# Spreading a one-channel image with GpSimd, its chain over three engines, in the last layer of a fused kernel

## The chip, the cores and the metric

The kernel runs on one core of a Trainium2 chip. The metric is device time in microseconds (us) of one execution of the whole program, which holds four network layers. A core has TensorE (matmul, PE in the profile), VectorE (DVE), ScalarE (ACT), GpSimd (POOL) and SyncE (SP), which here issues nearly all DMA transfers. Each engine runs its instructions in the order of its own stream and waits on semaphores for the others. SBUF is the on-chip memory; PSUM is the small memory that TensorE writes to.

## The reference, cut to what matters

The input x has the shape (1, 256, 256, 128), float32. Each of four layers computes `x = x + layer(gn(x))`, where gn is a group norm. Layer 0 is triangle attention, layers 1 and 2 are triangle multiplications, and layer 3 is the convolution layer that the change touches:

```python
def c1(t):   # nine taps along a row, 128 channels -> 1 channel
    return lax.conv_general_dilated(t, w1, (1, 1), 'SAME', dimension_numbers=DN) + b1
w2c = w2[0, 4]
def c2(t):   # one 128x128 product per pixel
    return jnp.einsum('bhwc,cd->bhwd', t, w2c) + b2
t = relu(c1(x))
y = jnp.concatenate([x[:, :1], x[:, 1:] + t[:, :-1]], axis=1)
u = relu(c1(y))
z_main = u + jnp.roll(y, 1, axis=1)
z = jnp.concatenate([z_main[:, :H - 2], u[:, H - 1:H] + y[:, H - 2:H - 1], y[:, H - 1:H]], axis=1)
v = relu(c2(z))
p = jnp.concatenate([z[:, :, :1], z[:, :, 1:] + v[:, :, :-1]], axis=2)
r = relu(c2(p))
q_main = r + jnp.roll(p, 1, axis=2)
q = jnp.concatenate([q_main[:, :, :W - 2], r[:, :, W - 1:W] + p[:, :, W - 2:W - 1], p[:, :, W - 1:W]], axis=2)
return q
```

t and u have one channel. So z is the normalized x, moved down by one row, plus a one-channel image e = u + (t moved by rows) that is added to all 128 channels of a pixel.

## The kernel before, in words

The last layer keeps channels on the 128 partitions and pixels along the free axis. The 256 rows are cut into 32 chunks of R = 8 rows (2048 pixels). x arrives from DRAM (`x3T`), 1 MB per chunk, by `load9` (L1461), with nine buffers. One step s of the main loop (`for s in range(NR + 2)`) works on several chunks at once:

- `taps(s + 6)`: TensorE multiplies the chunk by the nine taps (p9_pp, L1467), ScalarE copies the result out of PSUM (p9_st, L1471), and SyncE stores it to DRAM (sD, four stores).
- The image works on blocks of 16 rows, two chunks, hence over two steps. `load_block` (L1486, odd steps) reads the taps back from sD in a layout that has rows over all partitions (p9_S). `sum_taps` (even steps) adds the nine shifted taps (L1506) into `acc`, whose one part gives t (add b1, mask by `inside`, relu: L1508, L1509) and whose other part is kept for u. `keep_t` stores t to DRAM (tD), `image_u` forms u from nine products of t and `wsum` (p9_prod, L1523 to L1527), `load_t` (L1516, at the start of the odd step) reads t back moved by a row, `image_e` (odd steps) adds u and that and stores e to DRAM (eD). `load_e` (L1544, at the start of the next even step, behind `load9`) reads the rows of e for two chunks, four loads of 4 KB, into one of two tiles p9_er.
- `start_z(s + 1)`: ScalarE writes the scaled and shifted x into the SBUF tile p9_z (L1554). `finish_z(s + 1)`: TensorE broadcasts the row of e to all partitions with `broadcast_rows` (four matmuls with a 0/1 selector, p9_eb in PSUM, L1087), and VectorE adds it to p9_z in two halves (L1568).
- `p_half(s)`, twice: TensorE's product of z with w2c (p9_pm, L1574) and VectorE's max and add (p9_pb, L1582). `q_half(s - 1)`, twice: the same product of p, and VectorE's L1596 and L1599 into p9_q. p9_q starts as a scaled copy of x made by ScalarE (L1673), and GpSimd's `residual` (L1588 to L1590) adds p moved by one column. ScalarE adds two single columns (L1671 in p9_pb, L1688 in p9_q).
- `emit(s - 2)`: sixteen TensorE transposes (p9_pt, L1611), two ScalarE copies (L1612), and one 1 MB store to the output (L1613).

The order on every engine is the program's order (`tc.manual_schedule()`): no planner moves instructions. SyncE issues all these transfers from one queue in that order and stops at the first whose data is not ready. PSUM is shared: p9_pp, p9_eb and p9_pt take turns in one pool of two buffers, `psX` (tag "x"); p9_pm has two buffers of its own.

Ahead of the loop, the first chunks and block 0 go through the whole chain, and steps 0 and 1 each take a block (`begin_image`, `end_image`) from start to end.

Of the kernel before, what the change touches and what calls it, by code (L numbers as in the profile page):

```python
# [16 lines left out]
P = 128  # L17
N = 256
# [14 lines left out]
def kernel(ctx: ExitStack, tc: tile.TileContext, a: dict, out: bass.AP):  # L33
# [1417 lines left out]
    with tc.tile_pool(name="p9", bufs=2) as sb, tc.tile_pool(name="p9psM", bufs=2, space=PSUM) as psM, tc.tile_pool(  # L1451
# [4 lines left out]
        ers = [sb.tile([P, CK], F32, name=f"p9_er{i}", bufs=1) for i in range(2)]  # L1456
# [6 lines left out]
        def taps(x, h0, n):  # L1463
# [6 lines left out]
            st = sb.tile([P, 2, N], F32, name="p9_st", bufs=3)  # L1470
# [31 lines left out]
        def sum_taps(b):  # L1502

            k = blocks[b]
            k["acc"] = sb.tile([P, 2 * BW + 8], F32, name="p9_acc")
            nc.vector.tensor_reduce(k["acc"], k["St"].rearrange("p k w -> p w k"), AX.X, ALU.add)  # L1506
            k["t"] = sb.tile([P, BW + 8], F32, name="p9_t")
            nc.vector.scalar_tensor_tensor(k["t"], k["acc"][:, BW:], b1, inside, ALU.add, ALU.mult)  # L1508
            nc.vector.tensor_scalar(k["t"], k["t"], 0.0, None, ALU.max)  # L1509
# [8 lines left out]
        def image_u(b):  # L1518
            k = blocks[b]
            t = k["t"][:, 0:BW]  # L1520
            nine = bass.AP(tensor=t.tensor, offset=t.offset, ap=[list(t.ap[0]), [1, BW], [1, TAPS]])
            prod = sb.tile([P, BW, TAPS], F32, name="p9_prod", bufs=1)
            nc.vector.tensor_tensor(prod, nine, wsum.unsqueeze(1).to_broadcast([P, BW, TAPS]), ALU.mult)  # L1523
            k["u"] = sb.tile([P, BW], F32, name="p9_u")
            nc.vector.tensor_reduce(k["u"], prod, AX.X, ALU.add)
            nc.vector.tensor_tensor(k["u"], k["u"], k["acc"][:, 0:BW], ALU.add)
            nc.vector.tensor_scalar(k["u"], k["u"], b1, 0.0, ALU.add, ALU.max)  # L1527

        def image_e(b):
            k = blocks.pop(b)  # L1530
            e = sb.tile([P, BW], F32, name="p9_e")
            nc.vector.tensor_tensor(e, k["u"], k["t2"], ALU.add)
            if b < NB - 1:
                nc.sync.dma_start(image_rows(eD, b * BR), e)
            else:
                nc.sync.dma_start(image_rows(eD, N - BR, BR - 2), e[0 : P - 16, :])
                nc.sync.dma_start(image_rows(eD, N - 2, 1), e[P - 8 : P, :])
                nc.sync.dma_start(image_rows(eD, N - 1, 1), k["t"][P - 8 : P, 4 : 4 + BW])

        def load_e(b):  # L1540

            e_chunks = eD.rearrange("o (s c h w) -> c (o s) h w", c=4, h=2, w=NP)
            for c in range(4):
                nc.sync.dma_start(  # L1544
                    ers[b % 2][32 * c : 32 * c + 2, :].rearrange("s (h w) -> s h w", h=2),
                    e_chunks[c, 2 * b : 2 * b + 2, :, 4 : 4 + N],
                )

        def start_z(s):

            zs[s] = sb.tile([P, R, N], F32, name="p9_z", bufs=3)

            def take(lo, hi, src):
                nc.scalar.activation(zs[s][:, lo:hi, :], src, AF.Identity, bias=k0, scale=r3)  # L1554

            take(0, 1, xs[s - 1][:, R - 1 : R, :] if s else xe[:, 1:2, :])
            if s + 1 < NR:
                take(1, R, xs[s][:, 0 : R - 1, :])
            else:
                take(1, R - 2, xs[s][:, 0 : R - 3, :])  # L1560
                take(R - 2, R, xs[s][:, R - 2 : R, :])

        def finish_z(s):
            eb = broadcast_rows(psX, ers[s // 2 % 2], s % 2, "p9_eb")
            zf = zs[s].rearrange("p h w -> p (h w)")
            for h in range(2):
                hs = slice(h * H2, (h + 1) * H2)
                nc.vector.tensor_tensor(zf[:, hs], eb[h], zf[:, hs], ALU.add)  # L1568
# [52 lines left out]
        for er in ers:  # L1621
            nc.gpsimd.memset(er, 0.0)
# [36 lines left out]
        for s in range(4, 8):  # L1659
            load9(s)  # L1660
        finish_z(0)
        for s in range(NR + 2):
            load9(s + 8)
            b = s // 2 + 2
            if s % 2 == 1 and 2 < b < NB:
                load_t(b)
            if s % 2 == 0 and 3 < b <= NB:
                load_e(b - 1)
            if s < NR:
                pbs[s] = sb.tile([P, R, N], F32, name="p9_pb")  # L1670
# [39 lines left out]
            if s > 1:  # L1710
                emit(s - 2)

# [181 lines left out]
```

## Time and profile before

| what | value |
|---|---|
| median of 4 runs | 3350.22 us (3349.19 to 3358.12) |
| profiled execution | 3355.72 us, span 3354.0, mean granted TensorE clock 0.958 |
| busy over the whole span | TensorE 3090.4 us (92%), VectorE 2269.7 (68%), ScalarE 2018.6 (60%), GpSimd 1661.2 (50%) |
| TensorE's share of the chain that ended last | 40% of the span (DMA 4%, VectorE 2%, GpSimd 2%) |
| first p product, p(0) | starts at 2958.94 us |
| last copy of an output tile | ends at 3345.4 us |

The busy shares are means over four layers with different limits. What the changed stage is limited by has to be read from its own stretch, roughly 2920 to 3354 us. The chain that ended last is followed back from the last instruction: each row says when a piece began, how long it lasted and on what engine, tensor and line it was. A group of instructions gives engine, line, output and inputs, the number, busy time, the mean time of one in ns, and the idle time before it with what ended that. SyncE's rows are issues of transfers: a long one is an issue that had to wait.

### The profile page before, as it was taken

Reading aid. Unit: us, or ns where it says so; the run is one execution under the profiler, and the core shown is the slowest. Engines: PE = TensorE matmul, PEld = TensorE weight load, DVE = VectorE, ACT = ScalarE, POOL = GpSimd, SP = SyncE. Lnnn points to the kernel's source line nnn. Section 1 sums busy time; section 2 is a strip of 40 time slices with the busy share of each in tenths; the row PEclk is TensorE's granted clock in tenths of the full one; section 3 lists DMA queues with packets and bytes.
Section 4 is the critical chain, followed back from the end, with each engine's and each line's share of the span. In section 5 each row is a group of like instructions: output and inputs, shape, how many; then the busy total and the mean of one; then the engine's idle time right before and its main releaser. Section 6 shows DMA issues by size and latency. Waiting matters only on the chain.

```text
span 3354.0 us, 52187 instructions
## 1 busy us (share of the span) xinstructions
PE 3090.4 (92%) x20036; PEld 1644.1 (49%) x20036; DVE 2269.7 (68%) x2613; ACT 2018.6 (60%) x2209; POOL 1661.2 (50%) x904
## 2 busy tenths in 40 slices
PE   5668999999999999967996999999999999769998
PEld 4515555555555555532532444444899633224444
DVE  5626888888888888862555544545455688757776
ACT  3576777777777777734586544543444477736665
POOL 4055777777777777740385000000455588624444
PEclk7799999999999999989997999999999999879999
DMA  9982333333333333359599676865899899756764
GB/s 356 353 320 95 117 110 121 109 118 106 122 109 121 109 115 115 110 197 382 173 375 366 229 287 229 306 259 201 338 351 353 315 385 388 313 162 194 209 189 133
DMA packets 297908, 749.48 MB, mean 223 GB/s; under 512 B 74551, under 2 KB 145161, under 8 KB 248473
## 3 DMA queue, kind: packets, MB, share of 16 engines
q1 hardware_dynamic: 289719, 735.49, 61.3%
q0 software_dynamic: 7648, 9.55, 0.8%
q8 instruction: 161, 2.64, 0.3%
q10 hardware_dynamic: 288, 1.05, 0.1%
q14 instruction: 92, 0.75, 0.1%
HBM read 458.34 MB, written 287.64 MB: 222 GB/s over the span
## 4 chain that ended last, share of the span: by engine, by line
PE 40%; DMA 4%; DVE 2%; POOL 2%; issue 1%; ACT 1%; SPq 0%; ACTq 0%; DVEq 0%; POOLq 0%
PE p_pm L1172 13%; PE tp_z L1852 7%; PE p_pm L1335 6%; PE p_pm L1574 5%; PE tp_a L1841 2%; PE p_st L1129 2%; PE p_pt L1611 1%; POOL x L1035 1%; PE p_rk L1087 1%; PE p_pg L987 1%; PE p_eb L1087 1%; DMA p_er<-eD 1%; PE p_pz L1014 1%; PE p_pp L1467 1%; DMA p_x<-x3T 1%
## 5 line engine op out<-in xcount | busy, mean ns | idle before, releaser
L565 DVE TENSOR_TENSOR p_e<-p_S,triT 128x1024 f32<-128x1024 f32 x512 | 609.4, 1212 | 144.4 <-PE p_S L555 144.4
L575 POOL TENSOR_TENSOR p_es<-p_e 128x1024 f32<-128x1024 f32 x256 | 603.7, 2369 | 125.3 <-issue 64.9
L573 ACT ACTIVATE p_e<-p_e,mbT 128x1024 f32<-128x1024 f32 x512 | 552.0, 1138 | 61.4 <-DVE p_e L565 61.3
L1172 PE MATMUL p_pm<-p_zn,wf 128*128 128x512 f32 x1040 | 449.2, 593 | 2.7 <-ACT p_a L1207 1.9
L540 PE MATMUL p_mm<-p_xn,w 128*128 128x512 f32 x768 | 405.3, 611 | 0.3 <-DVE p_v L535 0.3
L1172 PEld LDWEIGHTS p_pm<-p_zn,wf 128*128 128x128 f32 x1040 | 196.7, 190 | 255.3 <-issue 247.8
L555 PE MATMUL p_S<-p_q,p_k 32*128 32x256 f32 x4096 | 295.5, 401 | 3.5 <-DVE p_e L565 3.3
L1588 POOL TENSOR_TENSOR p_q<-p_q,p_pb 128x2024 f32<-128x2024 f32 x32 | 144.2, 4505 | 253.3 <-DVE p_pb L1582 253.3
L555 PEld LDWEIGHTS p_S<-p_q,p_k 32*128 32x128 f32 x4096 | 186.0, 184 | 159.5 <-PE p_mm L531 91.7
L514 POOL TENSOR_TENSOR p_xn<-p_xn,p_rs 128x1024 f32<-128x1024 f32 x63 | 151.3, 2401 | 205.4 <-DMA p_rb<-rzD 146.2
L1262 POOL MEMSET k<- 128x512 f32 x1 | 0.5, 521 | 508.4 <-DVE p_zn L1165 508.4
L1852 PE MATMUL tp_z<-p_B,tp_at 128*128 128x256 f32 x1024 | 250.4, 388 | 0.8 <-DMA p_B<-bD 0.5
L588 PE MATMUL p_o<-p_e,p_v 128*32 128x256 f32 x4096 | 248.6, 383 | 0.0
L1293 POOL TENSOR_TENSOR k<-k,p_sq 128x512 f32<-128x512 f32 x128 | 163.2, 1275 | 159.2 <-ACT p_sq L1291 159.2
L1852 PEld LDWEIGHTS tp_z<-p_B,tp_at 128*128 128x128 f32 x1024 | 185.1, 191 | 23.2 <-DVE tp_at L1843 1.6
L540 PEld LDWEIGHTS p_mm<-p_xn,w 128*128 128x128 f32 x768 | 126.0, 190 | 104.6 <-issue 88.5
L1292 DVE TENSOR_TENSOR k<-tp_z,k 128x512 f32<-128x512 f32 x128 | 88.6, 692 | 127.0 <-ACT p_sq L1291 127.0
L588 PEld LDWEIGHTS p_o<-p_e,p_v 128*32 128x32 f32 x4096 | 120.3, 110 | 110.3 <-ACT p_g L546 41.5
L1289 ACT COPY p_K<-tp_z 128x512 f32<-128x512 f32 x128 | 75.1, 586 | 157.9 <-PE tp_z L1852 157.9
L546 ACT ACTIVATE p_g<-p_mm,bgh 128x512 f32<-128x512 f32 x128 | 88.0, 687 | 131.3 <-PE p_mm L540 131.3
L531 PEld LDWEIGHTS p_mm<-w,p_xn 128*128 128x128 f32 x1024 | 134.4, 191 | 61.1 <-issue 60.4
L544 ACT ACTIVATE p_k<-p_mm,cqkg 128x512 f32<-128x512 f32 x128 | 88.0, 688 | 125.1 <-PE p_mm L540 124.9
(376 smaller groups left out, 5989.9 us busy)
## 6 DMA issues: line engine op xcount, KB each, us to landing
p_x<-x2T SPq DMA_DIRECT2D x60, 1024.0 KB
x<-x1T SPq DMA_DIRECT2D x51, 1024.0 KB
p_x<-in_x_dram SPq DMA_DIRECT2D x32, 1024.0 KB
p_x<-xT SPq DMA_DIRECT2D x64, 512.0 KB
x2T<-x SPq DMA_DIRECT2D x32, 1024.0 KB
aD<-p_a SPq DMA_DIRECT2D x32, 1024.0 KB
bD<-p_b SPq DMA_DIRECT2D x32, 1024.0 KB
p_A<-aD SPq DMA_DIRECT2D x32, 1024.0 KB
```

The costliest lines, as they stand in the source:

```text
L514: nc.gpsimd.tensor_tensor(xn, xn, groups[g]["rs"], ALU.mult)
L540: nc.tensor.matmul(pm, lhsT=w, rhs=t["xn"][:, cs_], start=True, stop=True)
L555: nc.tensor.matmul(Ss[h // 2][:, h % 2, u, :], lhsT=t["k"][hp, r * N + u * P : r * N + (u + 1) * P], rhs=t["q"][hp, r * N : (r + 1) * N], ...
L565: nc.vector.tensor_tensor(e[:, :, 2 * p : 2 * p + 2, :].rearrange("p u h n -> p h u n"), Ss[p], triT[:, 2 * p : 2 * p + 2, :, :], ALU.add,)
L573: nc.scalar.activation(e[:, u, :, :], e[:, u, :, :], AF.Exp, bias=mbT[:, u, i : i + 1])
L575: nc.gpsimd.tensor_tensor(es, e[:, 0, :, :], e[:, 1, :, :], ALU.add)
L588: nc.tensor.matmul(t["o"][hp, r % 2, :], lhsT=t["v"][:, r * 2 + u, hp], rhs=e[:, u, h, :], start=(u == 0), stop=(u == 1),)
L1172: nc.tensor.matmul(pm[:, c, :], lhsT=wf2[:, i, :], rhs=zns[s][:, k * CK : (k + 1) * CK], start=True, stop=True)
L1293: nc.gpsimd.tensor_tensor(k2, k2, sq, ALU.add)
L1335: nc.tensor.matmul(pm[:, c, :], lhsT=w, rhs=src[:, k * CK : (k + 1) * CK], start=True, stop=True)
L1574: nc.tensor.matmul(pm[:, 2 * c : 2 * c + 2, :], lhsT=w2c, rhs=src[:, r : r + 2, :], start=True, stop=True)
L1852: nc.tensor.matmul(pz[:, t, :], lhsT=at[:, u, t * P : (t + 1) * P], rhs=Bc[:, u, :], start=(u == 0), stop=(u == 1))
```

## The change: what it does

- ScalarE's `start_z` writes to PSUM (p9_zp, two psX buffers, in pieces of 256, 768 and 1024 elements for an ordinary chunk) instead of p9_z. GpSimd's `partition_broadcast` spreads the row of e (2048 elements) to all partitions in an SBUF tile p9_eb (one buffer), called by `spread_e(s + 2)` behind `residual(s)`. VectorE's `finish_z` adds both into p9_z. The matmuls of `broadcast_rows` for e go, and the two p9_er tiles with their clearing become one tile with a row at partition 0, 32, 64 or 96; `load_e` makes two loads of 8 KB instead of four of 4 KB.
- The image chain is divided over three engines. VectorE: two reductions in `sum_taps` (41 and 33 columns of results, the second into a tenth column of p9_prod) and one over ten columns in `image_u`. ScalarE: the relus (`relu_t`, `relu_u`). GpSimd: the mask and the product (`shift_t`), and the sum e (`image_e`).
- `keep_t` and `load_t` now follow each other at the start of the odd step, `keep_e` and `load_e` at the start of the even step, ahead of its `load9`. So each load's issue comes directly behind the store that it must wait for.
- `start_z(s + 1)` comes before the first writing of p9_q, and the column of p9_q (L1688) comes at the end of the step's order on ScalarE.
- p9_st has two buffers instead of three, p9_acc one.

```diff
@@ -1453,7 +1453,8 @@
     ) as psX, tc.manual_schedule():
         x3r = x3T.rearrange("d (h w) -> d h w", w=N)
         xs, zs, pbs, qs, blocks = {}, {}, {}, {}, {}
-        ers = [sb.tile([P, CK], F32, name=f"p9_er{i}", bufs=1) for i in range(2)]
+        er = sb.tile([P, SC], F32, name="p9_er", bufs=1)
+        ebs, zps = {}, {}
 
         def load9(s):
             if s < NR:
@@ -1467,7 +1468,7 @@
                 nc.tensor.matmul(
                     pp[32 * c : 32 * c + 32, 0, :], lhsT=w1f, rhs=x[:, 2 * c : 2 * c + 2, :], start=True, stop=True
                 )
-            st = sb.tile([P, 2, N], F32, name="p9_st", bufs=3)
+            st = sb.tile([P, 2, N], F32, name="p9_st")
             nc.scalar.activation(
                 st[0 : 32 * n].rearrange("p h w -> p (h w)"), pp[0 : 32 * n, 0, :], AF.Identity, bias=s0[0 : 32 * n]
             )
@@ -1502,11 +1503,25 @@
         def sum_taps(b):
 
             k = blocks[b]
-            k["acc"] = sb.tile([P, 2 * BW + 8], F32, name="p9_acc")
-            nc.vector.tensor_reduce(k["acc"], k["St"].rearrange("p k w -> p w k"), AX.X, ALU.add)
+            St = k["St"].rearrange("p k w -> p w k")
+            k["acc"] = sb.tile([P, BW + 8], F32, name="p9_acc", bufs=1)
+            k["prod"] = sb.tile([P, BW, TAPS + 1], F32, name="p9_prod", bufs=1)
+            nc.vector.tensor_reduce(k["acc"], St[:, BW:, :], AX.X, ALU.add)
+            nc.vector.tensor_reduce(k["prod"][:, :, TAPS], St[:, 0:BW, :], AX.X, ALU.add)
+
+        def relu_t(b):
+            k = blocks[b]
             k["t"] = sb.tile([P, BW + 8], F32, name="p9_t")
-            nc.vector.scalar_tensor_tensor(k["t"], k["acc"][:, BW:], b1, inside, ALU.add, ALU.mult)
-            nc.vector.tensor_scalar(k["t"], k["t"], 0.0, None, ALU.max)
+            nc.scalar.activation(k["t"], k["acc"], AF.Relu, bias=b1)
+
+        def shift_t(b):
+            k = blocks[b]
+            nc.gpsimd.tensor_tensor(k["t"], k["t"], inside, ALU.mult)
+            t = k["t"][:, 0:BW]
+            nine = bass.AP(tensor=t.tensor, offset=t.offset, ap=[list(t.ap[0]), [1, BW], [1, TAPS]])
+            nc.gpsimd.tensor_tensor(
+                k["prod"][:, :, 0:TAPS], nine, wsum.unsqueeze(1).to_broadcast([P, BW, TAPS]), ALU.mult
+            )
 
         def keep_t(b):
             nc.sync.dma_start(image_rows(tD, b * BR + 1), blocks[b]["t"][:, 4 : 4 + BW])
@@ -1517,19 +1532,21 @@
 
         def image_u(b):
             k = blocks[b]
-            t = k["t"][:, 0:BW]
-            nine = bass.AP(tensor=t.tensor, offset=t.offset, ap=[list(t.ap[0]), [1, BW], [1, TAPS]])
-            prod = sb.tile([P, BW, TAPS], F32, name="p9_prod", bufs=1)
-            nc.vector.tensor_tensor(prod, nine, wsum.unsqueeze(1).to_broadcast([P, BW, TAPS]), ALU.mult)
             k["u"] = sb.tile([P, BW], F32, name="p9_u")
-            nc.vector.tensor_reduce(k["u"], prod, AX.X, ALU.add)
-            nc.vector.tensor_tensor(k["u"], k["u"], k["acc"][:, 0:BW], ALU.add)
-            nc.vector.tensor_scalar(k["u"], k["u"], b1, 0.0, ALU.add, ALU.max)
+            nc.vector.tensor_reduce(k["u"], k["prod"], AX.X, ALU.add)
+
+        def relu_u(b):
+            k = blocks[b]
+            nc.scalar.activation(k["u"], k["u"], AF.Relu, bias=b1)
 
         def image_e(b):
+            k = blocks[b]
+            k["e"] = sb.tile([P, BW], F32, name="p9_e")
+            nc.gpsimd.tensor_tensor(k["e"], k["u"], k["t2"], ALU.add)
+
+        def keep_e(b):
             k = blocks.pop(b)
-            e = sb.tile([P, BW], F32, name="p9_e")
-            nc.vector.tensor_tensor(e, k["u"], k["t2"], ALU.add)
+            e = k["e"]
             if b < NB - 1:
                 nc.sync.dma_start(image_rows(eD, b * BR), e)
             else:
@@ -1537,35 +1554,45 @@
                 nc.sync.dma_start(image_rows(eD, N - 2, 1), e[P - 8 : P, :])
                 nc.sync.dma_start(image_rows(eD, N - 1, 1), k["t"][P - 8 : P, 4 : 4 + BW])
 
+        def row_e(s):
+            at = 32 * (s % 4)
+            return er[at : at + 1, :]
+
         def load_e(b):
 
-            e_chunks = eD.rearrange("o (s c h w) -> c (o s) h w", c=4, h=2, w=NP)
-            for c in range(4):
+            for s in range(2 * b, 2 * b + 2):
                 nc.sync.dma_start(
-                    ers[b % 2][32 * c : 32 * c + 2, :].rearrange("s (h w) -> s h w", h=2),
-                    e_chunks[c, 2 * b : 2 * b + 2, :, 4 : 4 + N],
+                    row_e(s).rearrange("o (h w) -> o h w", w=N),
+                    eD.rearrange("o (h w) -> o h w", w=NP)[:, s * R : (s + 1) * R, 4 : 4 + N],
                 )
 
+        def spread_e(s):
+            if s < NR:
+                ebs[s] = sb.tile([P, SC], F32, name="p9_eb", bufs=1)
+                nc.gpsimd.partition_broadcast(ebs[s], row_e(s))
+
         def start_z(s):
 
+            zps[s] = [psX.tile([P, H, N], F32, name="p9_zp", tag="x") for _ in range(2)]
+
+            def take(lo, hi, src):
+                h = lo // H
+                nc.scalar.activation(zps[s][h][:, lo - h * H : hi - h * H, :], src, AF.Identity, bias=k0, scale=r3)
+
+            take(0, 1, xs[s - 1][:, R - 1 : R, :] if s else xe[:, 1:2, :])
+            take(1, H, xs[s][:, 0 : H - 1, :])
+            if s + 1 < NR:
+                take(H, R, xs[s][:, H - 1 : R - 1, :])
+            else:
+                take(H, R - 2, xs[s][:, H - 1 : R - 3, :])
+                take(R - 2, R, xs[s][:, R - 2 : R, :])
+
+        def finish_z(s):
             zs[s] = sb.tile([P, R, N], F32, name="p9_z", bufs=3)
-
-            def take(lo, hi, src):
-                nc.scalar.activation(zs[s][:, lo:hi, :], src, AF.Identity, bias=k0, scale=r3)
-
-            take(0, 1, xs[s - 1][:, R - 1 : R, :] if s else xe[:, 1:2, :])
-            if s + 1 < NR:
-                take(1, R, xs[s][:, 0 : R - 1, :])
-            else:
-                take(1, R - 2, xs[s][:, 0 : R - 3, :])
-                take(R - 2, R, xs[s][:, R - 2 : R, :])
-
-        def finish_z(s):
-            eb = broadcast_rows(psX, ers[s // 2 % 2], s % 2, "p9_eb")
-            zf = zs[s].rearrange("p h w -> p (h w)")
-            for h in range(2):
+            zf, eb = zs[s].rearrange("p h w -> p (h w)"), ebs.pop(s)
+            for h, zp in enumerate(zps.pop(s)):
                 hs = slice(h * H2, (h + 1) * H2)
-                nc.vector.tensor_tensor(zf[:, hs], eb[h], zf[:, hs], ALU.add)
+                nc.vector.tensor_tensor(zf[:, hs], zp.rearrange("p h w -> p (h w)"), eb[:, hs], ALU.add)
 
         def product9(src, h):
             pm = psM.tile([P, H, N], F32, name="p9_pm")
@@ -1618,8 +1645,6 @@
         nc.sync.dma_start(xe, x3r[:, N - 2 : N, :])
         for s in range(4):
             load9(s)
-        for er in ers:
-            nc.gpsimd.memset(er, 0.0)
         S0 = sb.tile([P, TAPS, 2 * BW + 8], F32, name="p9_S")
         nc.vector.memset(S0, 0.0)
 
@@ -1639,16 +1664,22 @@
         blocks[-1] = dict(St=S0)
         load_block(0)
         sum_taps(-1)
+        relu_t(-1)
+        shift_t(-1)
         nc.sync.dma_start(image_rows(tD, 0, 1), blocks.pop(-1)["t"][P - 8 : P, 4 : 4 + BW])
 
         def begin_image(b):
             sum_taps(b)
+            relu_t(b)
+            shift_t(b)
             keep_t(b)
             load_t(b)
 
         def end_image(b):
             image_u(b)
+            relu_u(b)
             image_e(b)
+            keep_e(b)
             load_e(b)
 
         begin_image(0)
@@ -1658,21 +1689,25 @@
         load_block(1)
         for s in range(4, 8):
             load9(s)
+        spread_e(0)
         finish_z(0)
+        spread_e(1)
         for s in range(NR + 2):
+            b = s // 2 + 2
+            if s > 3 and s % 2 == 0 and b <= NB:
+                keep_e(b - 1)
+                load_e(b - 1)
             load9(s + 8)
-            b = s // 2 + 2
-            if s % 2 == 1 and 2 < b < NB:
+            if s > 1 and s % 2 == 1 and b < NB:
+                keep_t(b)
                 load_t(b)
-            if s % 2 == 0 and 3 < b <= NB:
-                load_e(b - 1)
             if s < NR:
                 pbs[s] = sb.tile([P, R, N], F32, name="p9_pb")
                 nc.scalar.activation(pbs[s][:, :, 0:1], zs[s][:, :, 0:1], AF.Identity, bias=kcol[:, 0:1])
+                if s + 1 < NR:
+                    start_z(s + 1)
                 qs[s] = sb.tile([P, R, N], F32, name="p9_q", bufs=3)
                 nc.scalar.activation(qs[s], xs[s], AF.Identity, bias=kcol[:, 2:3])
-                if s + 1 < NR:
-                    start_z(s + 1)
                 p_half(s, 0)
                 p_half(s, 1)
                 del xs[s]
@@ -1685,30 +1720,33 @@
             if 0 < s <= NR:
                 q_half(s - 1, 0)
                 q_half(s - 1, 1)
-                nc.scalar.activation(
-                    qs[s - 1][:, :, N - 1 : N], qs[s - 1][:, :, N - 1 : N], AF.Identity, bias=kcol[:, 1:2]
-                )
                 del pbs[s - 1], zs[s - 1]
             if s < NR:
                 residual(s)
+                spread_e(s + 2)
             if s < 2:
 
                 for i in range(2):
                     taps(xs[4 + 2 * s + i], (4 + 2 * s + i) * R, 4)
                 load_block(s + 2)
             elif b < NB:
-                if s % 2 == 0:
-                    sum_taps(b)
-                    keep_t(b)
-                    image_u(b)
-                else:
-                    image_e(b)
+                sum_taps(b) if s % 2 == 0 else image_u(b)
             if s > 1 and s + LEAD < NR:
                 taps(xs[s + LEAD], (s + LEAD) * R, 4)
             if s > 1 and s % 2 == 1 and b + 1 < NB:
                 load_block(b + 1)
             if s > 1:
                 emit(s - 2)
+                if b < NB:
+                    if s % 2 == 0:
+                        relu_t(b)
+                        shift_t(b)
+                    else:
+                        relu_u(b)
+                        image_e(b)
+            if 0 < s <= NR:
+                last = qs[s - 1][:, :, N - 1 : N]
+                nc.scalar.activation(last, last, AF.Identity, bias=kcol[:, 1:2])
 
 
 def general_attention(tc, d, w, dram, stats1):
```

More of the change, by code (lines that the diff above doesn't have):

```diff
@@ L1549, in start_z @@
+        def spread_e(s):
+            if s < NR:
+                ebs[s] = sb.tile([P, SC], F32, name="p9_eb", bufs=1)
+                nc.gpsimd.partition_broadcast(ebs[s], row_e(s))
         def start_z(s):
-            zs[s] = sb.tile([P, R, N], F32, name="p9_z", bufs=3)
+            zps[s] = [psX.tile([P, H, N], F32, name="p9_zp", tag="x") for _ in range(2)]
             def take(lo, hi, src):
-                nc.scalar.activation(zs[s][:, lo:hi, :], src, AF.Identity, bias=k0, scale=r3)
+                h = lo // H
+                nc.scalar.activation(zps[s][h][:, lo - h * H : hi - h * H, :], src, AF.Identity, bias=k0, scale=r3)
@@ L1565, in finish_z @@
-            zf = zs[s].rearrange("p h w -> p (h w)")
-            for h in range(2):
+            zs[s] = sb.tile([P, R, N], F32, name="p9_z", bufs=3)
+            zf, eb = zs[s].rearrange("p h w -> p (h w)"), ebs.pop(s)
+            for h, zp in enumerate(zps.pop(s)):
                 hs = slice(h * H2, (h + 1) * H2)
-                nc.vector.tensor_tensor(zf[:, hs], eb[h], zf[:, hs], ALU.add)
+                nc.vector.tensor_tensor(zf[:, hs], zp.rearrange("p h w -> p (h w)"), eb[:, hs], ALU.add)
```

## The prediction

> **What bounds the kernel now.** I read the times and the whole page first. The profiled execution took 3355.72 us (span 3354.0 and 1.72 around it), 5.5 above the median of 3350.22. TensorE is busy for 92% of the span, and only the last layer, from about 2920 us on, is changed. So I read that stage in four views: the chain of waits, the groups of instructions, SyncE's queue, and the clock after idle time. The chain (start, length, what) shows two neighbouring steps of the main loop, the second one disturbed:
>
> ```profile
> 3114.14 3.44 PE p_pm L1574 x8
> 3117.58 1.07 PE p_eb L1087 x8
> 3118.65 3.63 PE p_pm L1574 x8
> 3122.28 1.00 PE p_pp L1467 x8
> 3123.28 1.74 PE p_pt L1611 x15
> 3125.02 5.08 DMA p_er<-eD
> 3130.23 1.62 PE p_eb L1087 x7
> 3131.84 5.33 PE p_pm L1574 x8
> 3137.17 1.00 PE p_pp L1467 x8
> 3138.16 1.91 PE p_pt L1611 x16
> ```
>
> An undisturbed step is all TensorE: 3.44 + 1.07 + 3.63 + 1.00 + 1.90 = 11.04 us, 22.08 for a pair. The disturbed one waits for the load of e (p_er), and its next products take 5.33 instead of 3.63. The product p(s) of step s starts at 3009.43 for s = 3, 3079.71 for 9, 3267.03 for 25 and 3328.13 for 31. From 9 to 25 a pair therefore lasts 187.32 / 8 = 23.4 us, 1.3 over the undisturbed pair.
>
> The groups of that stage (window 2800 to 3354; busy us, mean ns, idle before) give the prices:
>
> ```profile
> L1588 POOL TENSOR_TENSOR p_q<-p_q,p_pb 128x2024 f32<-128x2024 f32 x32 | 144.2, 4505 | 253.3 <-DVE p_pb L1582 253.3
> L1568 DVE TENSOR_TENSOR p_z<-p_eb,p_z 128x1024 f32<-128x1024 f32 x64 | 75.3, 1219 | 22.7 <-ACT p_z L1554 13.0 <-PE p_eb L1087 9.7
> L1087 PE MATMUL p_eb<-p_er,sel 32*128 32x512 f32 x256 | 42.3, 654 | 20.3 <-DMA p_er<-eD 18.1 <-ACT p_z L1554 2.1
> L1329 POOL PARTITION_BROADCAST p_rb<-rs__17908 x10 | 22.9, 2295 | 0.7
> L1590 POOL TENSOR_TENSOR p_q<-p_q,p_pb 128x8 f32<-128x8 f32 x32 | 7.3, 227 | 0.0
> ```
>
> The fourth is an operation that the change adds, in another stage. The third shows 20.3 us of TensorE idle before the broadcasts, 18.1 of it for the load of e.
>
> SyncE's queue in one pair (start, busy, what) shows the order of the transfers:
>
> ```profile
> 3084.14 0.41 SPq L1613 DMA_DIRECT2D out_dram<-p_o  x1
> 3084.59 1.84 SPq L1461 DMA_DIRECT2D p_x<-x3T  x1
> 3086.52 1.18 SPq L1516 DMA_DIRECT2D p_t<-tD  x1
> 3092.87 0.32 SPq L1534 DMA_DIRECT2D eD<-p_e  x1
> 3093.28 1.38 SPq L1476 DMA_DIRECT2D sD<-p_st  x4
> 3095.97 1.03 SPq L1486 DMA_DIRECT2D p_S<-sD  x2
> 3097.10 0.85 SPq L1613 DMA_DIRECT2D out_dram<-p_o  x1
> ```
>
> eD is held from 3087.70 to 3092.87: the small t2 load (p_t) lands only behind a 1 MB output and a 1 MB x, about 8.5 us after the output's issue. A small transfer behind large ones is late, and everything later in the queue waits too.
>
> **Part 1: the broadcast leaves TensorE.** The four matmuls (8 records) of a chunk, 1.07 us on the chain, go. A step's floor is 3.44 + 3.63 + 1.00 + 1.90 = 9.97 us; 8.97 without taps. GpSimd takes over: 2.295 per chunk by L1329. After each of those stood a gap of 1.17 to 1.25, which the wait for p_g explains; bounds of the added price 0 and 1.2, and I take 0, as the row is the same operation on the same shape. GpSimd's step: residual 4.505 + 0.236 + 0.227 = 4.97, broadcast 2.3, half of the image work. By L1588 against L1590, an element costs (4505 - 227) / (2024 - 8) = 2.12 ns, so the 297-element product takes 0.21 + 0.63 = 0.84, the mask 0.3, the e add 0.27: 0.7 per step. Sum 8.0, 9.2 with the extra: under 9.97. spread_e(s+2) stands behind residual(s), a whole step ahead of finish_z(s+2), so nothing waits for it in the steady state.
>
> The page "GPSIMD Engine Reference" of the Trainium skill (sections 3 and 4.1) speaks against this placement: two-input elementwise work belongs on VectorE, as GpSimd is about twice as slow. L1523, the same product on VectorE, took 0.469, against 0.84 estimated. By the page's factor it would be 0.94; either adds 0.4 to 0.5 us per pair to an engine with 2 us to spare per step, and nothing to the sum.
>
> **Part 2: ScalarE and VectorE.** z goes to PSUM in three pieces instead of two (0.4 + 1.9 becomes 0.4 + 0.8 + 1.0, by 1229 ns for a mean of two), and the two relus add 0.3 each per pair (as L1688, 301 ns). ScalarE's step: 0.32 + 2.3 + 2.0 + 0.69 + 2.03 + 0.3 + 0.3 = 7.9. VectorE loses the small image work and keeps z 2.4, pb 2.55, q 2.97 and about 0.95 of reductions: 8.9. Both under 9.97. Moving start_z ahead of the q initialisation gives z earlier (13.0 us of L1568's idle was for it); the q column at the end of the order is read only by the transposes a step later. The zp pair holds both psX buffers until finish_z: that ends about 7.1 after p starts (pb by 4.7, then 2 x 1.2), as the taps come due at 7.07 and the transposes at 8.07. Cost 0, within 0.5.
>
> VectorE's small two-input operation L1508 once took 3.40 us beside L1588 instead of 0.26. No operation with two SBUF inputs is left on VectorE in the loop: that stall in the start-up goes.
>
> **Part 3: stores and their loads on SyncE, the new wait.** The t2 load stands directly behind the tD store, the er loads behind the eD store, so SyncE stands still until each store has landed. Queued behind: taps' stores, loads of the taps, x, and output. The cycle of a pair, from an output's issue in an even step:
> - output, x, tD: before, t2 landed 8.5 after the output's issue at the same place. The even step's x load is issued only 1.8 before that output, so some of it is still under way: up to 0.8 more. Taken 9.3.
> - t2, four sD, their landing: 0.3 + 1.38 + 1.26 (the last sD issue to the p_S issue) + 0.2 = 3.1.
> - p_S (two loads, 1.03), output 0.85, eD: p_S packets last 1.9 and the output's 4.0, start 0.95 after the issue, and a small store needs 0.5 at its end (1.45 alone, less the 0.95): 7.3 to 7.4; 7.3.
> - two er loads 0.6, x 0.4, four sD 1.4: 2.4 to 2.5.
>
> Sum 22.2 us per pair, over TensorE's floor of 19.94. So the queue, not TensorE, becomes the bound, and TensorE idles 2.3 us a pair. Bounds: 20.5 (no leftover x, and each store 0.3 quicker) and 24.6 (each of the four landings 0.6 later, half the spread of the er stalls, 5.1 to 5.7, on each side doubled).
>
> TensorE idle of 1.65 us at 3059.07 was followed by a granted clock of 0.57 in this row (window 3060 to 3064):
>
> ```profile
> 3060.00:3064.00 4.00, 4.00 (x10) 1.51 (x5) 2.36 (x2) 0.00 (x0) 4.00 (x3) 0.57 0.74 216
> ```
>
> Such a step is 1.7 us longer (5.33 against 3.63). In a queue-bound pair 19.94 + 1.7 = 21.6 still fits into 22.2, so I charge nothing; if it did not hide, 8 pairs x 1.7 = 14.
>
> The page "TensorE: Matmul & The Clock Gate" (Part 1) says that the clock falls after an idle window of about 3.4 us. By the page idle of 2.3 us would cost nothing at all; the row above shows 1.65 to be enough. The sum is the same by both, the slow rival differs.
>
> **Part 4: start-up.** The p9_st buffers go from 3 to 2: the second chunk's taps wait for the first's stores, landed at about 2941.0, + 2.3. taps(2) and taps(3) now wait behind finish_z(0), as start_z(0) holds both psX buffers, and stand ahead of p(0): the image chain 0 passes through ScalarE and GpSimd (four handovers, 0.2 each) and two broadcasts of 2.3 come in, of which one is ahead of z(0). p(0) is about 6 later. tD(1) is queued behind x loads that start later, and the broadcast of chunk 2 behind residual(0). Against it stands the 3.4 us stall. p(3): + 4 to + 8, taken + 6. The tail, without image work, stays.
>
> **Sum.** Steps 3 to 9: the lead of the image is not yet used up; 6 x 9.97 = 59.8 against 70.3: - 10.5. Steps 9 to 25: 8 x 22.2 = 177.6 against 187.3: - 9.7. Steps 25 to 31: two more at 11.1, four at 8.8 to 8.97, 57.4 against 61.1: - 3.7. Start-up + 6, and 1.5 for the broadcast's extra price where it is exposed (between 0 and 5). Total - 16.4: 3355.7 becomes 3339.3, and taken off the median, 3334.
>
> **The rivals.**
> - TensorE stays the bound (queue quick enough, cycle at most 19.9). For: the transfers occupy only about 72% of the DMA time. Against: the order of the queue makes four landings serial. Steps 9 to 25 take 159.5 (- 27.8), 25 to 31 about 55 (- 6), 3 to 9 - 10.5, start-up + 4: - 40, 3310.
> - Slower: the queue cycle exceeds 24.5. One mechanism: each store waits behind a megabyte of other traffic, and its wait blocks the traffic that would refill the queue. For: eD's hold of 5 us above. Against: p_S and output are short enough by their packets. At 24.6, steps 9 to 25 take 196.8 (+ 9.5), 3 to 9 gain only 6, 25 to 31 gain 2, start-up + 8: + 9.5, 3360. It decides from about 23.6 on, where the other gains and the start-up cancel.
> - No net change: cycle 23.2. Steps 9 to 25 - 1.7, 3 to 9 - 8, 25 to 31 - 3, start-up and broadcast + 9.5: - 3, 3347.
>
> **How the numbers follow.** Queue-bound gain as summed 0.43, TensorE-bound 0.14, no net change 0.16, slower 0.27. A measurement tells about 0.2% (6.7 us) from no change: 3343.5 to 3357 is "same". Faster 0.57, same 0.15, slower 0.28. The likeliest case by itself spans 3322 to 3343; the range over the cases is 3314 to 3364.
>
> **What would show it.** Right: no p_eb on TensorE, L1574 pairs about 22 us apart, SyncE waiting for tD and eD stores in every pair, TensorE idle about 2 us per pair before p or the transposes, p(3) 4 to 8 us later. Wrong: idle before finish_z put down to the broadcast, a GpSimd busy over 10 us a step, pairs at 20 or above 23.5, or a half clock that adds to the pair.

## The result, and the profile after

The changed kernel takes 3356.74 us in the median (3348.25 to 3362.98, 32 runs) against 3350.85 (52 runs) before: ratio 1.0014 over all runs, 95% interval [1.0008, 1.0019]. That is within the 0.2% named as no change, but the interval excludes 1: a small loss, where a gain of 16.4 was forecast. The prediction said 3334.

Medians of the whole program hide where the time went, because the layers ahead of the changed stage also vary between executions: in the two profiles the stage begins 6.7 us apart. So the stage is cut at the starts of the products p(s) on TensorE and measured from the norm's last instruction (the reciprocal, L210), which ends the statistics that the stage needs. All numbers are us, from the profiled executions (span 3354.0 before, 3350.0 after):

| stretch | before | predicted after | after |
|---|---|---|---|
| L210 to p(3) | 81.8 | 87.8 | 87.2 |
| p(3) to p(9) | 70.3 | 59.8 | 65.0 |
| p(9) to p(25) | 187.3 | 177.6 | 194.8 |
| the same per pair of steps | 23.42 | 22.2 | 24.35 |
| p(25) to p(31) | 61.1 | 57.4 | 56.4 |
| p(31) to the end | 25.9 | 25.9 | 25.7 |
| stage | 426.3 | | 429.1 |

Steps 3 to 9 gain 5.3 and steps 25 to 31 gain 4.7; the start-up loses 5.4 and the loop 7.5. The stage is 2.8 longer in these two executions, while the medians are 5.9 apart; the other 3.1 is not traced to a place.

The chain of waits of this profile breaks off after three pieces, so TensorE's timeline takes its place (start, length, line, operation; in brackets the idle time before and what ended it):

```profile
3109.42 3.60 PE L1601 MATMUL p_pm<-p_z,w2c 128*128 128x512 f32 x8
3112.86 3.60 PE L1601 MATMUL p_pm<-p_pb,w2c 128*128 128x512 f32 x8
3116.39 1.06 PE L1468 MATMUL p_pp<-p_x,w1f 128*32 128x512 f32 x8
3117.38 1.97 PE L1638 MATMUL p_pt<-ident,p_q 128*128 128x128 f32 x16
3119.19 3.60 PE L1601 MATMUL p_pm<-p_z,w2c 128*128 128x512 f32 x8
3123.69 3.70 PE L1601 MATMUL p_pm<-p_pb,w2c 128*128 128x512 f32 x8 [0.90 <-DVE p_pb L1609]
3130.84 1.06 PE L1468 MATMUL p_pp<-p_x,w1f 128*32 128x512 f32 x8 [3.44 <-DVE p_z L1595]
3132.06 3.59 PE L1638 MATMUL p_pt<-ident,p_q 128*128 128x128 f32 x16 [0.16 <-DVE p_z L1595]
```

The broadcast is gone from TensorE and an undisturbed step is 9.77 us (3109.42 to 3119.19), so TensorE's floor is 19.54 a pair, a little under the predicted 19.94. But in every pair the taps (L1468) wait for z. The groups of the stage (window 2800 to 3354; busy us, mean ns, idle before) say for what, one link after the other:

```profile
L1595 DVE TENSOR_TENSOR p_z<-p_zp,p_eb 128x1024 f32<-128x1024 f32 x64 | 75.2, 1217 | 49.8 <-POOL p_eb L1572 49.8
L1572 POOL PARTITION_BROADCAST p_eb<-p_er x32 | 73.5, 2296 | 60.9 <-DMA p_er<-eD 46.6 <-ACT p_q L1710 6.2 <-DVE p_pb L1609 3.7
L1468 PE MATMUL p_pp<-p_x,w1f 128*32 128x512 f32 x256 | 42.2, 745 | 74.6 <-DVE p_z L1595 65.4 <-DMA p_x<-x3T 9.2
```

TensorE waits for z, z for the broadcast, the broadcast for the load of e. Before, TensorE waited for that load 18.1 us; now it is 46.6 on GpSimd. SyncE's queue shows why it is late, one pair from an even step's output to the next (t2 is the load of t back from tD, er the load of e's rows; a transfer lands when it is reported done):

```profile
3103.93 0.41 SPq L1640 DMA_DIRECT2D out_dram<-p_o  x1
3104.43 3.68 SPq L1462 DMA_DIRECT2D p_x<-x3T  x1
3108.21 0.60 SPq L1527 DMA_DIRECT2D tD<-p_t  x1
3114.11 0.32 SPq L1531 DMA_DIRECT2D p_t<-tD  x1
3114.52 1.38 SPq L1477 DMA_DIRECT2D sD<-p_st  x4
3117.14 1.03 SPq L1487 DMA_DIRECT2D p_S<-sD  x2
3118.23 1.90 SPq L1640 DMA_DIRECT2D out_dram<-p_o  x1
3120.22 2.07 SPq L1551 DMA_DIRECT2D eD<-p_e  x1
3125.03 1.27 SPq L1564 DMA_DIRECT2D p_er<-eD  x2
3126.34 0.44 SPq L1462 DMA_DIRECT2D p_x<-x3T  x1
3126.89 1.37 SPq L1477 DMA_DIRECT2D sD<-p_st  x4
3128.31 0.41 SPq L1640 DMA_DIRECT2D out_dram<-p_o  x1
```

Apart from the landings (of tD before 3114.11, of sD before 3117.14, of eD before 3125.03) the rows follow each other without a gap: here SyncE never stands still for an engine's work. Between 3080 and 3267 it waited 42.5 us for tD's landing, 20.0 for eD's and 9.1 for sD's. The long x and eD issues were not waiting for data: e had been ready since 3116.17, and x's buffer was last read a step earlier. (The profile's view of waits puts 15.7 us of the x issues to the taps L1468, but those taps read another chunk.) The likely reading, not tested by itself, is that the queue was taking them slowly. The pair lasts 24.38 here. Over eight pairs from 3080 on, the means of the four legs are 10.32 (output to t2), 3.15 (t2 to p_S), 7.49 (p_S to er), 3.25 (er to output): 24.21.

### The profile page after: what moved, and what is told of

It reads as the page before. It is cut to its first block, busy times and chain, and to the rows that moved or that the text cites. A ratio compares the mean times of both kernels' runs of the same rounds, so it can differ in the third digit from the quotient of the medians.

```text
span 3350.0 us, 51718 instructions
## 1 busy us (share of the span) xinstructions
PE 3050.2 (91%) x19780; PEld 1635.6 (49%) x19780; DVE 2242.2 (67%) x2532; ACT 2039.4 (61%) x2274; POOL 1755.5 (52%) x984
## 5 line engine op out<-in xcount | busy, mean ns | idle before, releaser
L531 PEld LDWEIGHTS p_mm<-w,p_xn 128*128 128x128 f32 x1024 | 134.4, 191 | 61.1 <-issue 60.4
L1211 DVE SCALAR_TENSOR_TENSOR p_b<-p_pm,b2w,p_b 128x1024 f32<-128x1024 f32 x64 | 82.1, 1283 | 118.6 <-PE p_pm L1172 104.1
```

What stands on the lines that cost most here:

```text
L531: nc.tensor.matmul(pm[:, k * D : (k + 1) * D], lhsT=t["xn"][:, b * P : (b + 1) * P], rhs=wf[:, 2 * D : 3 * D], start=True, stop=True,)
```

## The experiments

Theory Q: the queue's chain of landings sets the pair. Theory G: the new chain er, GpSimd's broadcast, finish_z, taps sets it, however the queue runs. A pair is always taken from p(9) to p(25) of one profiled execution; a measured time is the median of two to eight runs.

### The store ahead of the x load

```diff
+            if s > 3 and s % 2 == 0 and b <= NB:
+                keep_e(b - 1)
+            if s > 1 and s % 2 == 1 and b < NB:
+                keep_t(b)
+            load9(s + 8)
             if s > 3 and s % 2 == 0 and b <= NB:
-                keep_e(b - 1)
                 load_e(b - 1)
-            load9(s + 8)
             if s > 1 and s % 2 == 1 and b < NB:
-                keep_t(b)
                 load_t(b)
```

> Edit: in each step the store (tD or eD) is issued ahead of the 1 MB x load and its load (t2 or er) behind it; nothing else. Theory Q (SyncE's queue of four serial landings sets the pair at 24.35 us between p(9) and p(25)): the x load is issued while the store lands, so the cycle shortens to about 3.2 (t2 issue to p_S issue) + 7.5 (p_S issue to er issue, x inside) + 8.3 (er, four sD, output, tD landing behind x and output) = 19.0, under TensorE's 19.94. Pair 20 to 21 us, p(9) to p(25) 160 to 168 instead of 194.8, time 3322 to 3332. Theory G (the chain er load, GpSimd's broadcast, finish_z, taps sets the pair, wherever the stores stand): pair 23.5 to 25, time 3350 or more, as er now lands behind x, later by 3.

Measured: pair 20.79, p(9) to p(25) 166.4, time 3319.72, ratio to the kernel before 0.9919 [0.9904, 0.9933]. Its queue:

```profile
3099.28 0.32 SPq L1531 DMA_DIRECT2D p_t<-tD  x1
3099.69 1.38 SPq L1477 DMA_DIRECT2D sD<-p_st  x4
3102.63 1.03 SPq L1487 DMA_DIRECT2D p_S<-sD  x2
3103.75 0.78 SPq L1640 DMA_DIRECT2D out_dram<-p_o  x1
3104.62 2.69 SPq L1551 DMA_DIRECT2D eD<-p_e  x1
3107.37 1.09 SPq L1462 DMA_DIRECT2D p_x<-x3T  x1
3111.10 1.27 SPq L1564 DMA_DIRECT2D p_er<-eD  x2
3112.47 1.49 SPq L1477 DMA_DIRECT2D sD<-p_st  x4
3114.01 0.41 SPq L1640 DMA_DIRECT2D out_dram<-p_o  x1
3116.16 0.34 SPq L1527 DMA_DIRECT2D tD<-p_t  x1
```

The x load is issued at 3107.37, inside the wait for eD, and SyncE has idle time of its own at 3114.42 to 3116.16, where it waits for t. Theory Q holds; for theory G the broadcast would have kept the pair at 23.5 or more, though nothing about it was changed. The exchanged order is worth 33 us in the stage of the profiled executions (429.1 - 396.0), or 37 by the medians, which were not taken side by side (3356.74 - 3319.72).

### Loads that wait for no store

```diff
-            nc.sync.dma_start(t2, image_rows(tD, b * BR))
+            away = x3T[0:1, 0 : P * BW].rearrange("o (p w) -> p (o w)", w=BW)
+            nc.sync.dma_start(t2, image_rows(tD, b * BR) if b < 3 else away)
...
-                    eD.rearrange("o (h w) -> o h w", w=NP)[:, s * R : (s + 1) * R, 4 : 4 + N],
+                    eD.rearrange("o (h w) -> o h w", w=NP)[:, s * R : (s + 1) * R, 4 : 4 + N]
+                    if b < 3
+                    else x3T[0:1, s * SC : (s + 1) * SC].rearrange("o (h w) -> o h w", w=N),
```

Both loads:

> Edit: from block 3 on, the t2 and er loads read as many bytes from x3T, which is long finished, instead of tD and eD; so e is not the image's from there on, but every transfer stays and no load waits for a store. Theory Q: SyncE never stands still for a landing of tD or eD, the pair falls to TensorE's floor, 19.9 to 20.3, p(9) to p(25) 159 to 163. Theory G (broadcast chain or GpSimd's order): pair still 23 or more, as the broadcast and everything behind it is unchanged.

Measured: pair 20.22, p(9) to p(25) 161.8, 3307.05 us. As theory Q expected: within 0.3 of the predicted floor of 19.94 and 0.7 over the measured 19.54, with GpSimd's work unchanged. By itself this run does not exclude a chain through the image's data, as e no longer depends on t here; the queue's rows above, in which SyncE waits for landings and no engine, do.

The t2 load alone:

> Edit: from block 3 on, only the t2 load reads from x3T instead of tD, so e is not the image's from there on; the er load still waits for the eD store. Theory Q: of the measured cycle 10.4 + 3.2 + 7.5 + 3.3 the first leg (an output's issue to t2's issue) falls to issue times and the queue's own fullness, about 5: cycle about 19 to 20, so the pair is 20 to 21. If each landing costs by itself, the two waits are worth about 5.5 each over the floor. Theory G: pair 23 or more.

Measured: pair 22.73, 3332.73 us. Neither theory's number: the gain is 1.6, not 3.4 or more. The queue shows where the rest went:

```profile
3102.09 0.47 SPq L1532 DMA_DIRECT2D p_t<-x3T  x1
3102.66 1.46 SPq L1477 DMA_DIRECT2D sD<-p_st  x4
3108.52 1.03 SPq L1487 DMA_DIRECT2D p_S<-sD  x2
```

From the last sD issue to p_S it is now 4.40, where the changed kernel has 1.24 (3115.90 to 3117.14). The taps' stores land behind the same output and x that tD had waited for, and p_S waits for them. The wait moved to the next landing.

The er load alone:

> Edit: from block 3 on, only the er load reads from x3T instead of eD, so what is spread is not e; the t2 load still waits for the tD store. Seen before: with the tD wait gone, p_S waited instead, since the taps' stores then landed behind output and x (4.4 us), and the pair fell only to 22.73. Theory Q now: SyncE runs from p_S to tD without a landing, but tD lands behind p_S, output, x, output, x: 0.95 + 1.9 + 3.8 + 3.5 + 3.8 + 3.5 + 0.5 = 17.9 after p_S's issue, and 3.1 from t2 to p_S: cycle 21.0, pair 20.6 to 21.8. If both waits cost alike: about 22.7. Theory G: 23 or more.

Measured: pair 22.16, 3333.89 us. A gain of 2.2, a little under what was expected (21.8 at most). Each single wait taken away gives 1.6 or 2.2; together they give 4.1.

### The broadcast twice

```diff
                 nc.gpsimd.partition_broadcast(ebs[s], row_e(s))
+                nc.gpsimd.partition_broadcast(ebs[s], row_e(s))
```

> Edit: GpSimd broadcasts each row of e twice into the same tile, 2.3 us more per chunk. Theory Q: GpSimd has 15.6 of 24.4 us busy in a pair, and the broadcast lies outside SyncE's cycle: 20.2 busy, pair 24.2 to 24.8, start-up + 2 to 5, time + 2 to 9. Theory G: the broadcast lies on the path once or twice per pair, pair 26.6 to 29, p(9) to p(25) 213 or more, time + 25 or more.

Measured: pair 24.03, so 2.3 us more in front of each z costs the loop nothing. The groups of 3073 to 3265:

```profile
L1596 DVE TENSOR_TENSOR p_z<-p_zp,p_eb 128x1024 f32<-128x1024 f32 x33 | 38.9, 1219 | 34.3 <-POOL p_eb L1573 34.0
L1573 POOL PARTITION_BROADCAST p_eb<-p_er x16 | 36.8, 2299 | 1.4
```

VectorE waits 34.0 us for the broadcast, and that is no proof that the broadcast is the bound: the idle time is named after the last link, and the pair is as long as without it. The time was 3369.06, 12 more than the changed kernel, where 2 to 9 had been expected. It is lost outside the loop: p(3) comes 6.8 later, p(3) to p(9) takes 3.2 more, and p(25) to p(31), where the image's transfers end, 7.3 more (63.7). So there the broadcast does count.

### Only the stores' places, in the kernel before

```diff
-            load9(s + 8)
             b = s // 2 + 2
-            if s % 2 == 1 and 2 < b < NB:
-                load_t(b)
             if s % 2 == 0 and 3 < b <= NB:
+                keep_e(b - 1)
                 load_e(b - 1)
+            load9(s + 8)
+            if s % 2 == 1 and 2 < b < NB:
+                keep_t(b)
+                load_t(b)
```

with `keep_e` split from `image_e`, and `keep_t` taken out of the even step, in lines not shown.

> Edit: the kernel before, with nothing of the change but the stores' places: tD at the start of the odd step behind the x load and directly ahead of the t2 load, eD at the start of the even step directly ahead of the er loads, ahead of the x load. Theory Q: the same queue cycle as after the change, 24.35, plus 0.7 for four er loads instead of two (2.0 against 1.27): pair 24.3 to 25.5 against 23.42, p(9) to p(25) 194 to 204, time + 7 to + 17 against the kernel before. Rival N (the stores' places do no harm by themselves; what the change lost comes from GpSimd's work): pair 23.0 to 23.8, time within 5.

Measured: pair 24.30, and 3348.04 us, ratio 1.0007 [0.9997, 1.0018]. Two rows of its queue on each side of the waits:

```profile
3103.79 0.45 SPq L1512 DMA_DIRECT2D tD<-p_t  x1
3108.92 0.32 SPq L1516 DMA_DIRECT2D p_t<-tD  x1
...
3113.97 2.42 SPq L1538 DMA_DIRECT2D eD<-p_e  x1
3119.72 1.14 SPq L1548 DMA_DIRECT2D p_er<-eD  x4
```

The loop is that of the changed kernel within 0.05 us a pair, with TensorE still broadcasting. So 24.3 belongs to the order of the stores and their loads, and in it the broadcast's move off TensorE is worth nothing. The time was expected 7 or more higher, and was not measurably higher: p(9) to p(25) lost 7.1, but p(3) to p(9) took 66.7 instead of 70.3 in the profiled executions.

### The broadcast back on TensorE, with the store ahead

The edit restores the two p9_er tiles, the four er loads, z in SBUF and `broadcast_rows` in the kernel of the first experiment:

```diff
+            eb = broadcast_rows(psX, ers[s // 2 % 2], s % 2, "p9_eb")
             zf = zs[s].rearrange("p h w -> p (h w)")
-            for h, zp in enumerate(zps.pop(s)):
+            for h in range(2):
                 hs = slice(h * H2, (h + 1) * H2)
-                nc.vector.tensor_tensor(zf[:, hs], zp.rearrange("p h w -> p (h w)"), eb[:, hs], ALU.add)
+                nc.vector.tensor_tensor(zf[:, hs], eb[h], zf[:, hs], ALU.add)
```

> Edit: the changed kernel with the store ahead of the x load, and the broadcast of e back on TensorE (p9_er, four loads of 4 KB, z written to SBUF, as before the change). Theory Q: the queue is no longer the bound, so the pair is TensorE's floor with the broadcast, 22.08, plus at most 0.8: 22.1 to 22.9, time 3335 to 3347. So spreading by GpSimd is worth 1.3 to 2 us a pair, once the queue allows. Rival: GpSimd's broadcast costs what TensorE's saves; then the pair is 20.8 to 21.2 as with GpSimd.

Measured: pair 22.07, TensorE's floor with the broadcast (22.08) to 0.01 us; 3329.04 us. The time is 6 below the range that was expected; the start-up is shorter, p(3) at 78.6 against 87.0 with GpSimd's broadcast. With the queue out of the way the move to GpSimd is worth 22.07 - 20.79 = 1.28 a pair, and costs 8.4 in the start-up as the change arranges it.

### Half an output store

```diff
-            nc.sync.dma_start(
-                out_tok[s * SC : (s + 1) * SC, :].rearrange("(k p) d -> p k d", p=P), ot
-            )
+            part = out_tok[s * SC : (s + 1) * SC, :].rearrange("(k p) d -> p k d", p=P)
+            if s < NR - 1:
+                nc.sync.dma_start(part[:, 0 : SC // P // 2, :], ot[:, 0 : SC // P // 2, :])
+            else:
+                nc.sync.dma_start(part, ot)
```

> Edit: the changed kernel, but each output store writes only the first half of its chunk (0.5 MB instead of 1 MB; the other half of the output is left unwritten); order and waits are untouched. Theory Q in its sharper form (a landing is late by the megabytes that stand in front of it): the output's packets shrink by 1.9 in each of two legs, cycle 24.35 - 3.8 = 20.5, pair 20.2 to 21.3. Rival L (a landing has a price of its own, whatever stands in front of it): pair 23.5 to 24.4.

Measured: pair 19.97, 3310.22 us. An even step's output and the one behind it:

```profile
3090.94 0.41 SPq L1642 DMA_DIRECT2D out_dram<-p_o  x1
...
3098.83 0.32 SPq L1531 DMA_DIRECT2D p_t<-tD  x1
...
3108.64 1.27 SPq L1564 DMA_DIRECT2D p_er<-eD  x2
...
3111.92 0.41 SPq L1642 DMA_DIRECT2D out_dram<-p_o  x1
```

Output to t2 is 7.89 here instead of 10.18. Over the first eight such pairs the means are 7.90 and 5.68 for the two legs that hold an output, 2.4 and 1.8 less, while t2 to p_S (3.15) does not move. So a landing is late by the bytes in front of it; the price per byte is not fixed by this one size, and with TensorE's floor so near the pair may have been held there.

### ScalarE's column, and the buffers of p9_st

On the kernel with the store ahead, the column back at its old place:

```diff
+                last = qs[s - 1][:, :, N - 1 : N]
+                nc.scalar.activation(last, last, AF.Identity, bias=kcol[:, 1:2])
                 del pbs[s - 1], zs[s - 1]
...
-            if 0 < s <= NR:
-                last = qs[s - 1][:, :, N - 1 : N]
-                nc.scalar.activation(last, last, AF.Identity, bias=kcol[:, 1:2])
```

> Edit: on top of the store ahead of the x load, ScalarE's column of p_q back at its old place, behind the q products' issue and ahead of taps' copy. With the queue out of the way this would show. GpSimd's residual of the step before ends about 2 us after p's start, and ScalarE would come to the column at about 6.4, so it waits for nothing: pair 20.6 to 21.0, within 0.2 of 20.79, time within 3 of the kernel it stands on. Rival: the column waits for GpSimd and holds up the taps' copies: pair 21.5 or more.

Measured: pair 20.71, 3318.78 us. It cost nothing, as charged.

```diff
-            st = sb.tile([P, 2, N], F32, name="p9_st")
+            st = sb.tile([P, 2, N], F32, name="p9_st", bufs=3)
```

> Edit: on top of the store ahead of the x load, p9_st with three buffers again. The prediction charged two buffers with + 2.3 in the start-up: p(0) at 33.0 to 34.0 after the norm's reciprocal instead of 35.7, p(3) at 84 to 85.5 instead of 87.0; the loop unchanged (20.79). Rival: the wait is hidden by the image chain of block 0, p(3) at 86.5 to 87.5.

Measured: p(0) at 33.8, p(3) at 84.7, pair 20.72. p(0) is 1.9 earlier than with two buffers and p(3) 2.3. The first is clear (seven profiles with the same start-up have p(0) at 35.7 to 36.3), the second hardly (p(3) at 85.7 to 88.9); in the time (3320.06) they are below what three runs can tell.

### The start-up

```diff
             taps(xs[s], s * R, 4)
-        start_z(0)
...
         load_block(0)
+        for s in range(2, 4):
+            taps(xs[s], s * R, 4)
         sum_taps(-1)
...
         begin_image(0)
+        start_z(0)
         end_image(0)
-        for s in range(2, 4):
-            taps(xs[s], s * R, 4)
         load_block(1)
```

with p9_st's three buffers and the store ahead of the x load.

> Edit: on top of the store ahead of the x load, the start-up: taps(2) and taps(3) stand behind load_block(0) and ahead of the image chain of block 0, start_z(0) between begin_image(0) and end_image(0), and p9_st has three buffers again. Theory on the start-up (p(0) 4.8 later through p9_st with two buffers and through taps(2), taps(3) behind finish_z(0)): p(0) at 30.5 to 32.5 after the norm's reciprocal instead of 35.7, p(3) at 82 to 84.5 instead of 87.0, time 2.5 to 5 less than without the edit, 3315 to 3317. Rival: the start-up is bound by x's loads and the image chain of blocks 1 and 2; p(3) stays at 86 to 88.

Measured: 3306.18 us, ratio to the kernel before 0.9878 [0.9862, 0.9895], the fastest version that computes the whole layer. p(0) comes at 33.1 (expected 30.5 to 32.5), but p(3) at 77.3, better than the 82 to 84.5 expected, and the loop keeps 20.60. The queue of the changed kernel (L210 at 2920.95) has

```profile
2961.64 3.30 SPq L1462 DMA_DIRECT2D p_x<-x3T  x5
2965.50 0.32 SPq L1527 DMA_DIRECT2D tD<-p_t  x1
2977.99 0.32 SPq L1531 DMA_DIRECT2D p_t<-tD  x1
```

and this kernel (L210 at 2919.5)

```profile
2949.37 3.16 SPq L1462 DMA_DIRECT2D p_x<-x3T  x5
2961.15 0.32 SPq L1527 DMA_DIRECT2D tD<-p_t  x1
2965.01 0.32 SPq L1531 DMA_DIRECT2D p_t<-tD  x1
```

With the taps' stores earlier, the five x loads are issued 10.8 earlier, and tD of block 1 no longer stands right behind them: it lands 3.9 after its issue instead of 12.5. So a small store behind large loads held the start-up as well. Over the run with three buffers alone, p(0) gains only 0.7 and p(3) 7.4, which the expectation had not foreseen.

## Why the prediction was wrong, point by point

- **The failed step is the sum of the queue's cycle in part 3.** The mechanism was right: the queue became the bound, and the landings of tD and eD hold it. The size was not: 22.2 predicted, 24.35 by p(9) to p(25). By legs, predicted and measured: 9.3 and 10.32 (output to t2), 3.1 and 3.15, 7.3 and 7.49, 2.5 and 3.25 (er to output). Two terms carry most of it. Two er loads took 1.27 to issue, not 0.6. And the 0.8 allowed for the x load still under way was too little, the first leg shows 1.8: before the tD store can land, x, output and x have to pass one after the other. From the output's issue to t2's, 3.09 MB moved (3128.3 to 3138.2). In the kernel before, whose 8.5 was the starting row, it was 2.15 MB (3084.1 to 3092.7), and the queue had just run nearly empty (21 GB/s from 3083 to 3084). The windows 3128 to 3132 and 3132 to 3136 after the change moved 311 and 373 GB/s (rows below), at which 3 MB last an estimated 8.4 to 10.1 us. The halved output shows that a landing gets later with the bytes in front.
- **That reversed the sign of the loop.** Steps 9 to 25 were to give - 9.7 and gave + 7.5, 17.2 of the 19.2 us between the forecast - 16.4 and the stage's + 2.8. The pair's upper bound of 24.6 held, and the slower rival, with its threshold of 23.6, describes the loop that came, mechanism included. Its likelihood (0.27) was low for a sum whose terms were taken from a queue that was less full.
- **Steps 3 to 9** were to run at TensorE's floor, 59.8, on the image's lead; they took 65.0. Steps 3 to 6 do run at 9.77 each, then step 7 takes 15.69: the lead was used up sooner than assumed. With the store ahead steps 3 to 9 take 60.5, so it was the queue here too.
- **Start-up** + 6 predicted, + 5.4 measured, some 2 of it p9_st's buffers, as charged. The rest of the sum is not confirmed by its near total: in the last run, which takes tD(1) out from behind the x loads, p(3) comes 7.4 earlier, and the prediction had named that wait without giving it a price of its own. **p(25) to p(31)** - 3.7 predicted, - 4.7 measured. **Tail** unchanged, as said.
- **The prices of parts 1 and 2 held.** The broadcast took 2.296 (2.295 taken), GpSimd's product 0.812 (0.84), and no extra price of a broadcast appears in the loop: doubling it left the pair at 24.03. What did not hold in part 1 is that nothing waits for the broadcast in the steady state: z waited 49.8 us for it, since er came late, which the prediction had listed as a sign of being wrong. The column on ScalarE cost nothing; z waited for no ScalarE work any more, so its new order did what it was to do. "GPSIMD Engine Reference" of the Trainium skill (section 4.1) calls two-input elementwise work on GpSimd about twice as slow: the product took 0.812 against 0.469 on VectorE, 1.7 times, and it was hidden.
- **The half clock was mostly hidden, as charged.** In the timeline shown, the transposes at 3132.06 take 3.59 instead of 1.97, in the second of these rows of the windows (busy time of PE, PEld, DVE, ACT, POOL, then the granted clock, DMA share and GB/s):

```profile
3128.00:3132.00 4.00, 1.06 (x8) 0.16 (x8) 2.44 (x3) 0.03 (x1) 3.84 (x4) 1.00 0.88 311
3132.00:3136.00 4.00, 3.94 (x18) 3.73 (x19) 2.94 (x5) 1.98 (x3) 3.90 (x4) 0.57 1.14 373
```

  Yet that pair of the queue (3128.31 to 3152.48) lasts 24.17, and the one before it, at full clock, 24.38. Of the eight pairs from 3080 on, five hold a stretch at half clock and last 24.4 in the mean (23.4 to 25.5), three hold none and last 23.9 (23.5 to 24.4). The difference is less than the 1.7 that a step loses, and lies inside the spread.

One thing stays open: with the store ahead, the pair is 20.79, 1.25 over the measured floor of 19.54, while VectorE still waits 13.4 us for the broadcast between 3073 and 3240. Whether the rest is the later er load was not tried.

## What to carry to other kernels

Where a load waits for a store in an in-order queue, try the next big, independent transfer between the two instead of in front of the store: the same transfers in another order were worth 3.6 us a pair here. When the price of a landing is estimated, count the bytes that will stand in front of it in the new order, not those of the old one; and when one wait is taken out, look at which landing in the queue is late by the same bytes. Idle time named after one engine (z waiting for the broadcast, 34 us) is not yet a bound; doubling that engine's work showed here that it was none.

## What the runs showed of the hardware that was not expected

- The length of TensorE's idle time alone does not settle the clock. In the kernel before, 1.65 us idle was followed by a clock of 0.57; after the change, 3.25 us idle (before 3106.43) was followed by transposes at their usual 1.94, and 3.44 us idle (before 3130.84) by 3.59. The page "TensorE: Matmul & The Clock Gate" of the Trainium skill (Part 1) puts the fall after an idle window of about 3.4 us; the 1.65 us do not fit that.
- After the change, from 3080 to 3274, the stretches at half clock begin at 3132.05, 3155.95, 3179.84, 3207.15 and 3251.52, and each lasts 3.41 us or twice that. The starts lie 7, 7, 8 and 13 times 3.41 us apart. So the clock changes on a fixed grid here; what in a span of the grid decides was not tested.
- Two er loads of 8 KB occupied SyncE for 1.27 us, four of 4 KB in the same place for 1.14 (1.9 to 2.0 in the kernel before, directly behind an x load): halving the number of these loads saved no issue time.
